# Scores three steps ahead of their values in the last cross attention, with six tiles of exponentials and a smaller arena

## The chip, the cores and the metric

The kernel runs on one core of one Trainium2 chip, in one launch. The metric is device time in microseconds; the kernel before takes 1653.15 us, the median of 3 runs (1653.11 to 1653.16). The engines are named as in the profile: PE is TensorE's matmuls, PEld its weight loads, DVE is VectorE, ACT is ScalarE, POOL is GpSimd, SP issues the transfers.

## The reference, cut to what matters

Four blocks follow each other on x of 8 batches x 112 rows x 256. Each attends to the same context of 8 x 375 x 192. All is in float32.

```python
x = L0(x, ctx)   # self attention, cross attention, gated GELU feed-forward; 16 heads of 64
x = L1(x, ctx)   # the same, other weights
x = L2(x, ctx)   # cross attention alone, 16 heads of 64
x = L3(x, ctx)   # decoder block, 16 heads of 16:
    # h = ln(x);  q, k, v = h @ qkv_w + qkv_b
    # a = softmax(where(causal | tgt_mask, -inf, q k^T * 0.25)); x += (a v) @ proj_w + proj_b
    # h = ln(x);  q = h @ q_w + q_b; k, v = ctx @ k_w + k_b, ctx @ v_w + v_b
    # a = softmax(where(enc_mask, -inf, q k^T * 0.25));          x += (a v) @ out_w + out_b
    # h = ln(x);  x += gelu(h @ mlp1_w + mlp1_b) @ mlp2_w + mlp2_b
```

## The kernel before, in words

The parts of the four blocks are numbered as stages 0 to 9: 0, 1, 2 are self attention, cross attention and feed-forward of the first block; 3, 4, 5 those of the second; 6 is the third block's cross attention; 7, 8, 9 are self attention, cross attention and feed-forward of the last. Attention is cut into *steps* (`add_step`, lines 913 to 1101). A step is a batch and some heads: in the cross stages four heads, so 32 steps a stage; in stage 7 eight heads, two steps a batch. The steps of stage 7 are woven between those of stages 6 and 8 (`after`, line 1194). In all there are 176 steps; step 138 is the first of stage 8 and step 175 the last.

A step has these items. "S" makes the scores on TensorE into two PSUM tiles "s" (a pool of two) and then issues the softmax. In stages 7 and 8 that is, for each head, a DVE instruction that adds the mask to the scores and takes the maximum (line 934; it writes the masked scores into an SBUF tile "pr" and the maximum into "nm"), and an exponential on ACT, in place (line 942). Half of a step's exponentials are issued with S, the other half in the item "E". "T" transposes the exponentials on TensorE, four heads to a bank, three banks in a cross step (line 1013), into PSUM tiles "mm" (a pool of four that every other product shares), and each bank is copied to an SBUF tile "wT": banks 0 and 2 by ACT (line 1022), bank 1 by DVE (line 1019). "PV" multiplies by the values (line 1043); two steps' PV stand together. After the last step of a batch, "R" and "N" scale the result by the sums. Step i uses two tiles of "pr"; the pool has four.

TensorE's instructions stay in the order in which the Python code emits them. That order is written by a planner (`Plan`). Its main loop (lines 1454 to 1495) goes step by step, and in loop step i it emits S(i+2), then the two PV if i is odd, then the banks of T(i+1), then E(i+2). Between these it puts *fill*: the other work (projections, layer norm transposes, feed-forward) by deadline, counted in steps, as soon as its inputs are there and there is room. `pace` says how much fill a step should take. The other engines' instructions follow each in its own queue, in an order close to that of emission.

Queries, keys and values live in one SBUF tile, the "arena", 12224 columns of float32 on 128 partitions. `Plan.find` gives each a place when its projection is emitted; a projection that finds no room has to wait. A cross stage with heads of 64 has for each batch eight keys of 375 columns and six values of 512.

The context masks of stage 8 are made on POOL ("mask" items, line 578); deadlines of queries (`q_deadline`), of the transposed layer norms "hT" (`hT_by`) and of the keys (`add_key_jobs`) are so many steps ahead of the step that uses them. The GELU of stage 9 is done for the feed-forward's first 512 rows and for the next 256 as separate ACT instructions over four banks of 512 or 256 columns (line 1325). They need another table of functions than the exponentials, so the first of them may only follow the last S in the plan:

```python
deps=[(("ff", st, f, m), 1.0) for m in range(8)] + [(("S", len(steps) - 1), 4.0)],
```

Of the kernel before, what the change touches and what calls it, by code (L numbers as in the profile page):

```python
# [15 lines left out]
B, T, D = 8, 112, 256  # L16
S, DC = 375, 192
# [46 lines left out]
def last_batch(t):  # L64
    return min(B - 1, (P * (t + 1) - 1) // T)
# [234 lines left out]
def kernel(ctx: ExitStack, tc: tile.TileContext, a: dict, out: bass.AP):  # L300
    nc = tc.nc
    PSUM = bass.MemoryType.PSUM
    RINGS = {"w": 7, "row": 2, "xn": 3}
    ARENA = 12224

    const = ctx.enter_context(tc.tile_pool(name="const", bufs=1))
    wpool = ctx.enter_context(tc.tile_pool(name="wpool", bufs=RINGS["w"]))
    rpool = ctx.enter_context(tc.tile_pool(name="rpool", bufs=RINGS["row"]))
    ppool = ctx.enter_context(tc.tile_pool(name="ppool", bufs=4))
    tpool = ctx.enter_context(tc.tile_pool(name="tpool", bufs=6))  # L310
    xpool = ctx.enter_context(tc.tile_pool(name="xpool", bufs=RINGS["xn"]))
    small = ctx.enter_context(tc.tile_pool(name="small", bufs=4))
# [4 lines left out]
    def mm_tile():  # L317
        return ps_m.tile([P, 512], F32, tag="mm", name="mm")

    arena = const.tile([P, ARENA], F32, name="arena")  # L320
    plan = Plan(RINGS, ARENA, lambda k: 512 if k[0] == "v" else S if k[0] == "k" and k[1] in (1, 4, 6, 8) else 4 * T)

    def place(key):

        lo, hi = plan.place[key]
        t = arena[:, lo:hi]
        return t if hi - lo != 4 * T else t.rearrange("p (i t) -> p i t", i=2)

    SEG = [0, 0, 0, 1, 1, 1, 2, 2, 2, 2]
# [216 lines left out]
    def add_masks():  # L546


        src = ("w", "m8")

        def load():
            m8 = wpool.tile([T, B * (T + S)], U8, tag="w", name="m8")
            nc.sync.dma_start(m8[:, : B * T], a["mask_BxS_bf0"].rearrange("b t -> (b t)").partition_broadcast(T))
            nc.sync.dma_start(m8[:, B * T :], a["mask_BxS2_bf0"].rearrange("b s -> (b s)").partition_broadcast(T))
            got[src] = m8

        def self_mask():
            nc.gpsimd.tensor_scalar_mul(cmask.rearrange("p b t -> p (b t)"), got[src][:, : B * T], NEG)
            nc.gpsimd.affine_select(
                cmask, cmask, pattern=[[0, B], [-1, T]], compare_op=ALU.is_ge, fill=NEG, base=0,  # L560
                channel_multiplier=1,
            )

        plan.add_load(Item(("load", "masks"), 0, load, makes=[src]))
        plan.add(Item(("mask", "self"), 0, self_mask, first_of(7, 0) - 8, uses=[src], seg=SEG[6]))
        yield
        for i in range(2):
            key = ("w", "cm", i)

            def place(i=i, key=key):  # L570
                got[key] = wpool.tile([T, 4, S], F32, tag="w", name="cm")

            plan.add_load(Item(("load", key), 0, place, makes=[key]))
            for n in range(4):

                def ctx_mask(i=i, n=n, key=key):
                    c = B * T + (4 * i + n) * S
                    nc.gpsimd.tensor_scalar_mul(got[key][:, n, :], got[src][:, c : c + S], NEG)

                b = 4 * i + n  # L580
                plan.add(Item(("mask", b), 0, ctx_mask, first_of(8, b) - 5, uses=[src, key], seg=SEG[7]))


    xns = {}
# [194 lines left out]
    def add_key_jobs(st, b, w, deadline, last=False):  # L779

        cols = slice(b * S, (b + 1) * S)
        wv = ("ctx", "k") if last else w
        rest = D if last else INNER
        for u in range(1 if last else 4):
            keys = [("k", st, b, 2 * u + i) for i in range(2)]
            cell = []

            def begin(u=u, cell=cell):
                for i in range(2):
                    ps = mm_tile()  # L790
                    nc.tensor.matmul(  # L791
                        ps[:, :S], lhsT=got[wv][:, (2 * u + i) * P : (2 * u + i + 1) * P], rhs=ctxA[:, cols],
                        start=True, stop=False,
                    )
                    cell.append(ps)

            def fn(u=u, keys=keys, cell=cell):
                for i in range(2):
                    r = slice(i * KB, (i + 1) * KB)
                    nc.tensor.matmul(  # L800
                        cell[i][:, :S], lhsT=got[wv][r, rest + u * P : rest + (u + 1) * P], rhs=ctxB[r, cols],
                        start=False, stop=True,
                    )
                for i in range(2):
                    t = place(keys[i])
                    evac(t, cell[i][:, :S], S, None, bcols[:, 6 + i : 7 + i] if last else None)
                    got[keys[i]] = t

            plan.add(Item(("kj", st, b, u), 2.1, fn, deadline(b, u), uses=[w], makes=keys, deps=ctx_deps(b),
                          seg=SEG[st], begin=begin))  # L810
# [36 lines left out]
    def ctx_deps(b):  # L847
        return [(("ctxT", b), 4.0)]
# [60 lines left out]
    at = {}  # L909
# [257 lines left out]
    def first_of(st, b):  # L1167
        return at[(st, b, 0)]

    def last_of(st, b):  # L1170
        return at[(st, b, per[st] - 1)]
# [6 lines left out]
        return lambda t: [(("N", st, last_batch(t)), 1.2)]  # L1178

    def q_deadline(st, j):  # L1180
        return first_of(st, 2 * j) - 3.4

    L0 = ("L0_xattn_", "Wq1 Wk1 Wv1 Wo1 bo1 g1 b1 Wq2 Wk2 Wv2 Wo2 bo2 g2 b2 Wp Wf bf g3 b3 bp".split())
    L1 = (
# [24 lines left out]
    def hT_by(st):  # L1209
        if st == 9:  # L1210
            return lambda gi: last_of(8, last_batch(GROUPS[gi][-1])) + 2.0
        if st in ff_at:
            return lambda gi: ff_at[st] - 0.5 + 0.02 * gi
        return lambda gi: first_of(st, (256 * gi) // T) - 4

    def norm_by(st):
        f = hT_by(st)
        if st == 9:
            return lambda t: last_of(8, last_batch(t)) + 1.4
        if st in ff_at:  # L1220
            return lambda t: f(t // 2) - 0.01
        return lambda t: f(t // 2) - 0.7
# [14 lines left out]
    def cross_stage(st, wq, wk, wv, qscale, vscale):  # L1237
        last = st == 8
        for j in range(4):
            if last:  # L1240
                add_last_projection(st, "q", j, wq, ("sq", "qc"), q_deadline(st, j), 2)
            else:
                add_pair_projection(st, "q", j, wq, 4, lambda j, u: q_deadline(st, j) + 0.01 * u, qscale)
        for b in range(B):

            add_key_jobs(st, b, wk, lambda b, u: at[(st, b, u)] - 3.0, last)
            if not last:
                add_value_jobs(st, b, wv, lambda b, i: at[(st, b, (0, 0, 2)[i])] - 1.5 + 0.1 * i, vscale)

        if last:  # L1250
            add_last_values(st, wv, lambda b: first_of(st, b) - 1.3)
# [102 lines left out]
    st = 0  # L1354
    for bi, (L, n) in enumerate(seq):
# [40 lines left out]
        if bi == 0:  # L1396
            add_context_transposes(lambda b: f1 + 4 * b - 5 if b > 1 else 7 + b)
        cross_stage(s1, w(n[7]), w(n[8]), w(n[9]), 0.125, None)
        add_products(s1, s2, w(n[10]), 8, after_pv(s1), norm_by(s2))
        add_norm_transposes(s2, n[17], n[18], hT_by(s2))  # L1400
# [50 lines left out]
    nc.vector.tensor_copy(vcols, pt0[:, :NVR])  # L1451
    plan.now = 7.0

    cuts = [0, ff_at[2], ff_at[5], ff_at[9]]
    for seg in range(3):
        lo, hi = cuts[seg], cuts[seg + 1]


        for s in (lo, lo + 1):
            for k in plan.items[("S", s)].uses + plan.items[("PV", s)].uses:  # L1460
                mk = plan.maker.get(k)
                if mk is None or plan.items[mk].done:
                    continue
                if plan.items[mk].begin is not None:
                    plan.require(mk)
                else:
                    plan.drain(mk)
        if seg == 0:
            plan.require(("hT", 0, 1))
        for i in range(lo - 2, hi):  # L1470
            plan.step = i
            left = plan.pace(i, seg)
            if i < lo:

                left = max(left, 6.5)
            plan.close_jobs()
            if lo <= i + 2 < hi:
                plan.main(("S", i + 2))

            if lo <= i < hi and (i - lo) % 2 == 1:  # L1480
                plan.main(("PV", i - 1))
                plan.main(("PV", i))
            if lo <= i + 1 < hi:
                n = steps[i + 1]
                share = left / (n + 2)
                left -= plan.fill(2 * share, 1.5 if i < lo else 0.0)
                for k in range(n):
                    plan.main(("T", i + 1, k))
                    left -= plan.fill(min(left, share))
            if ("E", i + 2) in plan.items and lo <= i + 2 < hi:  # L1490
                plan.main(("E", i + 2))
            plan.fill(left, 1.5 if i < lo else 0.0)


            plan.open_jobs(1 if i + 1 >= first_of(8, 0) or i + 2 in woven else 2, i + 3.5, seg)
# [38 lines left out]
```

## Time and profile before

| | |
|---|---|
| median of 3 runs | 1653.15 us |
| profiled execution: its own time | 1654.93 us |
| profiled execution: span from first to last instruction | 1653.1 us |
| busy: PE, PEld | 1633.3 us, 1141.0 us |
| busy: DVE, ACT, POOL | 812.8 us, 782.6 us, 718.5 us |
| granted TensorE clock, mean | 0.999 |
| step 138's scores start | 1423.9 us |
| step 175's scores start | 1603.5 us |

A line of a group reads: source line, engine, operation, out<-in with shapes, count, then busy us and mean ns of one, then idle time of the engine just before them and what ended it. A line of the waits reads: engine, tile and line that waited, what it waited for, then us in total, number of times, and the longest. A line of the timeline reads: start us, duration us, engine, line, operation, and in brackets the idle time before it with its releaser. A matmul's end in the profile is modelled, so a busy PE can hold short waits inside it; PEld, the weight load that precedes each matmul, often shows them better.

### The profile page before, as it was taken

How to read it: one execution, taken by the hardware profiler on the slowest of the kernel's cores; microseconds unless marked ns; L12 is line 12 of the kernel's file. 1: busy time of each engine (PE TensorE's matmuls, PEld its weight loads, DVE VectorE, ACT ScalarE, POOL GpSimd, SP SyncE). 2: the span in 40 equal slices, each digit the busy share in tenths (PEclk: the TensorE clock that was granted, in tenths of full speed). 3: DMA queues.
4: the chain of work that ended last, by engine and by line, in shares of the span. 5: the costliest groups of instructions: out<-in, count | busy, mean ns of one | idle time of the engine just before them, and what ended most of it. 6: DMA issues, size and time to landing. Idle time of an engine off the chain costs nothing.

```text
span 1653.1 us, 30104 instructions
## 1 busy us (share of the span) xinstructions
PE 1633.3 (99%) x11772; PEld 1141.0 (69%) x11772; DVE 812.8 (49%) x2164; ACT 782.6 (47%) x2450; POOL 718.5 (43%) x687
## 2 busy tenths in 40 slices
PE   9999999999999999999999999999999999999999
PEld 8777766666657878676666665675666666766667
DVE  3554454544532344545444552344455556677752
ACT  3453444444531445434444452144445555787772
POOL 1323555656632223355565570364564447422110
PEclk9999999999999999999999999999999999999999
DMA  6021020000101011000000010100000000000000
GB/s 187 5 66 42 3 87 1 1 26 1 52 29 46 1 29 52 27 1 30 1 2 26 1 46 30 33 23 1 1 2 1 16 2 26 30 2 1 2 2 23
DMA packets 26613, 39.50 MB, mean 24 GB/s; under 512 B 1527, under 2 KB 21623, under 8 KB 26471
## 3 DMA queue, kind: packets, MB, share of 16 engines
q1 hardware_dynamic: 26231, 37.40, 7.3%
q8 instruction: 93, 1.52, 0.4%
q14 instruction: 49, 0.40, 0.1%
q10 hardware_dynamic: 240, 0.17, 0.0%
HBM read 35.88 MB, written 0.92 MB: 22 GB/s over the span
## 4 chain that ended last, share of the span: by engine, by line
PE 91%; ACT 4%; DVE 3%; POOL 1%; issue 1%; ACTq 0%; POOLq 0%; DVEq 0%
PE mm L669 13%; PE mm L703 11%; PE mm L1043 10%; PE s L986 10%; PE mm L1013 9%; PE mm L791 8%; PE mm L825 7%; PE mm L1263 6%; PE mm L800 5%; PE mm L834 4%; PE mm L750 3%; ACT pr L942 2%; PE mm L1298 2%; PE mm L637 1%; ACT pr L954 1%
## 5 line engine op out<-in xcount | busy, mean ns | idle before, releaser
L963 POOL TENSOR_SCALAR pr<-pr,rinv 112x375 f32<-112x375 f32 x384 | 468.7, 1239 | 340.6 <-DVE rinv L960 340.6
L954 ACT ACTIVATE pr<-s,nm 112x375 f32<-112x375 f32 (+1 forms) x640 | 302.0, 490 | 168.7 <-DVE nm L948 166.5
L355 DVE COPY arena<-mm 128x375 f32<-128x375 f32 (+4 forms) x189 | 113.3, 609 | 287.8 <-PE mm L800 138.3
L1013 PEld LDWEIGHTS mm<-ident,pr 112*128 112x128 f32 (+2 forms) x1920 | 209.1, 151 | 48.1 <-issue 20.6
L1013 PE MATMUL mm<-ident,pr 112*128 112x112 f32 (+2 forms) x1920 | 234.7, 264 | 5.5 <-ACT pr L942 3.3
L347 ACT COPY arena<-mm 128x375 f32<-128x375 f32 (+4 forms) x179 | 92.8, 519 | 296.3 <-PE mm L800 140.9
L948 DVE TENSOR_REDUCE nm<-s 112x2 f32<-112x750 f32 (+1 forms) x224 | 206.3, 957 | 50.2 <-PE s L986 46.5
L986 PE MATMUL s<-arena 64*112 64x375 f32 (+3 forms) x1792 | 211.0, 394 | 0.1
L1043 PEld LDWEIGHTS mm<-wT,arena 128*64 128x64 f32 (+5 forms) x3840 | 160.5, 130 | 36.9 <-issue 19.0
L347 ACT COPY wT<-mm 119x448 f32<-119x448 f32 (+2 forms) x235 | 123.9, 536 | 124.5 <-PE mm L1013 124.4
L1043 PE MATMUL mm<-wT,arena 128*64 128x112 f32 (+5 forms) x3840 | 180.3, 262 | 0.0
L986 PEld LDWEIGHTS s<-arena 64*112 64x112 f32 (+1 forms) x1792 | 114.1, 172 | 80.4 <-issue 30.9
L942 ACT ACTIVATE pr<-pr,nm 112x112 f32<-112x112 f32 (+1 forms) x256 | 124.7, 491 | 32.0 <-DVE nm L934 32.0
L969 POOL TENSOR_TENSOR pr<-pr,rinv 112x896 f32<-112x896 f32 x32 | 53.9, 1685 | 197.5 <-DVE rinv L967 180.0
L954 ACT ACTIVATION_READ_ACCUMULATOR pr<-s,nm 112x1 f32 x640 | 133.3, 208 | 0.0
L599 POOL TENSOR_TENSOR rs<-ve,mhalf 128x1 f32<-128x1 f32 x70 | 39.7, 568 | 203.0 <-DVE ve L597 202.9
L960 DVE RECIPROCAL rinv<-sums 112x1 f32<-112x1 f32 x384 | 62.4, 163 | 90.1 <-ACT pr L954 89.6
L825 PE MATMUL mm<-L_xattn_Wv,ctxA 128*128 128x512 f32 (+1 forms) x192 | 92.5, 601 | 2.3 <-ACT wT L347 1.3
L791 PE MATMUL mm<-ctxA,L_xattn_Wk 128*128 128x375 f32 x256 | 92.0, 482 | 0.6 <-DVE wT L355 0.5
L673 DVE TENSOR_TENSOR x<-mm,x 128x256 f32<-128x256 f32 x70 | 29.6, 423 | 115.9 <-PE mm L669 115.9
L703 PE MATMUL mm<-hT,L_xattn_Wq 128*128 128x224 f32 x384 | 83.0, 360 | 0.0
L353 DVE TENSOR_SCALAR arena<-mm 128x448 f32<-128x448 f32 (+2 forms) x65 | 42.0, 646 | 82.0 <-PE mm L834 47.1
(134 smaller groups left out, 2323.7 us busy)
## 6 DMA issues: line engine op xcount, KB each, us to landing
L_xattn_Wo<-in_L_xattn_Wo_dram SPq DMA_DIRECT2D x3, 1024.0 KB, 15.8
L_xattn_w_ff<-in_L_xattn_w_ff_dram SPq DMA_DIRECT2D x3, 1024.0 KB, 5.2
L_xattn_Wv<-in_L_xattn_Wv_dram SPq DMA_DIRECT2D x4, 512.0 KB, 5.0
L_xattn_Wq<-in_L_xattn_Wq_dram SPq DMA_DIRECT2D x2, 1024.0 KB, 4.7
L_xattn_Wp<-in_L_xattn_Wp_dram SPq DMA_DIRECT2D x2, 1024.0 KB, 5.8
L_xattn_wq<-in_L_xattn_wq_dram SPq DMA_DIRECT2D x2, 1024.0 KB
L_xattn_wo<-in_L_xattn_wo_dram SPq DMA_DIRECT2D x2, 1024.0 KB, 5.2
L_xattn_mlp_w<-in_L_xattn_mlp_w_dram SPq DMA_DIRECT2D x2, 1024.0 KB, 5.4
```

Of the source, the lines that this page charges most:

```text
L347: nc.scalar.copy(dst, src)
L669: nc.tensor.matmul(ps[:, :D], lhsT=oT[:, c, t * P : (t + 1) * P], rhs=got[wv or w][:, c, :], start=(c == 0), stop=(c == n - 1),)
L703: nc.tensor.matmul(ps[:, i * 2 * T : (i + 1) * 2 * T], lhsT=got[w][:, k, m * P : (m + 1) * P], rhs=hT[:, k, lo:hi], start=(k == 0), stop=( ...
L791: nc.tensor.matmul(ps[:, :S], lhsT=got[wv][:, (2 * u + i) * P : (2 * u + i + 1) * P], rhs=ctxA[:, cols], start=True, stop=False,)
L825: nc.tensor.matmul(ps[: KCH[c][1], :], lhsT=lhs(ctxA, slice(0, KA), c), rhs=got[w][:, hf * 512 : (hf + 1) * 512], start=True, stop=False,)
L942: return nc.scalar.activation(pr, pr, AF.Exp, bias=nm, scale=-1.0, accum_out=bsums[(st, b)][:, h : h + 1])
L948: nc.vector.tensor_reduce(nm[:, :, :ns], sv, AX.X, ALU.max, negate=True)
L954: nc.scalar.activation(pr[:, bk, sl, :], sv[:, bk, sl, :], AF.Exp, bias=nm[:, bk, sl : sl + 1], accum_out=sums[:, bk, sl : sl + 1],)
L963: nc.gpsimd.tensor_scalar_mul(pr[:, bk, sl, :], pr[:, bk, sl, :], rinv[:, bk, sl : sl + 1])
L986: nc.tensor.matmul(tiles[i][:, n % 2, (n // 2) * nk : (n // 2 + 1) * nk], lhsT=qap(h), rhs=kap(h), start=True, stop=True,)
L1013: nc.tensor.transpose(pt[:kl, m * T : (m + 1) * T], cell[h][:, c * P : c * P + kl], ident[:T, :T])
L1043: nc.tensor.matmul(po[p0 : p0 + dp, blk * T : (blk + 1) * T], lhsT=got[vk][:kl, hv * dp : (hv + 1) * dp], rhs=wt, start=(c == 0 and par(h) ...
```

## The change

From loop step DEEP on (three before the first step of stage 8, so step 135) the planner emits S and E of step i+3 in loop step i instead of those of step i+2. On the first such step it emits both S(i+2) and S(i+3). In the stages before, nothing changes in this rule. For it the pool of "pr" tiles has six instead of four (a tile is 896 columns in its largest use), and the arena shrinks from 12224 to 10400 columns, in all stages. Deadlines of what stages 7 and 8 need before their scores are one step earlier: masks, queries, hT and keys.

```diff
-    ARENA = 12224
+    ARENA = 10400
...
-    ppool = ctx.enter_context(tc.tile_pool(name="ppool", bufs=4))
+    ppool = ctx.enter_context(tc.tile_pool(name="ppool", bufs=6))
...
-        plan.add(Item(("mask", "self"), 0, self_mask, first_of(7, 0) - 8, uses=[src], seg=SEG[6]))
+        plan.add(Item(("mask", "self"), 0, self_mask, first_of(7, 0) - 9, uses=[src], seg=SEG[6]))
...
-                plan.add(Item(("mask", b), 0, ctx_mask, first_of(8, b) - 5, uses=[src, key], seg=SEG[7]))
+                plan.add(Item(("mask", b), 0, ctx_mask, first_of(8, b) - 6, uses=[src, key], seg=SEG[7]))
...
     def q_deadline(st, j):
-        return first_of(st, 2 * j) - 3.4
+        return first_of(st, 2 * j) - (4.4 if st > 6 else 3.4)
...
-        return lambda gi: first_of(st, (256 * gi) // T) - 4
+        return lambda gi: first_of(st, (256 * gi) // T) - (5 if st > 6 else 4)
...
-            add_key_jobs(st, b, wk, lambda b, u: at[(st, b, u)] - 3.0, last)
+            add_key_jobs(st, b, wk, lambda b, u: at[(st, b, u)] - (4.0 if last else 3.0), last)
...
+    DEEP = first_of(8, 0) - 3
...
-            if lo <= i + 2 < hi:
-                plan.main(("S", i + 2))
+            ahead = 3 if seg == 2 and i >= DEEP else 2
+            due = [n for n in range(i + 2, i + ahead + 1) if lo <= n < hi and not plan.items[("S", n)].done]
+            for n in due:
+                plan.main(("S", n))
...
-            if ("E", i + 2) in plan.items and lo <= i + 2 < hi:
-                plan.main(("E", i + 2))
+            for n in due:
+                if ("E", n) in plan.items:
+                    plan.main(("E", n))
```

## The prediction

> **What bounds the kernel now.** I read the page first, then stretches of ten to thirty us of the last block, then who waits for whom in them, and last the instructions around two of the waits. Part 1 of the page gives busy time by engine, part 4 the chain that ended last:
>
> ```profile
> PE 1633.3 (99%) x11772; PEld 1141.0 (69%) x11772; DVE 812.8 (49%) x2164; ACT 782.6 (47%) x2450; POOL 718.5 (43%) x687
> PE 91%; ACT 4%; DVE 3%; POOL 1%; issue 1%; ACTq 0%; POOLq 0%; DVEq 0%
> ```
>
> TensorE bounds the whole; its matmul work is untouched by the change, so only time in which it stands can be won. The stretches (columns: busy us of PE, PEld, DVE, ACT, POOL, then granted clock) show where that is:
>
> ```profile
> 1424.00:1444.00 20.00, 19.31 (x208) 14.05 (x209) 15.24 (x56) 15.15 (x44) 8.15 (x10) 1.00 0.19 60
> 1444.00:1464.00 20.00, 18.84 (x209) 14.04 (x208) 16.30 (x73) 18.64 (x69) 4.45 (x9) 1.00 0.01 2
> 1564.00:1594.00 30.00, 30.00 (x234) 17.07 (x231) 15.25 (x53) 19.61 (x51) 3.42 (x7) 1.00 0.00 1
> 1594.00:1604.00 10.00, 9.24 (x115) 6.52 (x113) 7.78 (x27) 9.34 (x28) 0.25 (x1) 1.00 0.01 2
> 1604.00:1614.00 10.00, 8.19 (x133) 6.34 (x126) 5.38 (x18) 7.76 (x15) 2.92 (x4) 0.83 0.01 2
> ```
>
> ACT is at 93% in places (18.64 of 20), with room just before (15.15 of 20). TensorE's waits from 1424 to 1598 (stage 8 up to its last three steps), and for contrast those of stage 4:
>
> ```profile
> PE mm L1013 <- ACT pr L942: 2.0, 7, 0.4
> PE mm L791 <- ACT wT L1022: 1.1, 2, 0.6
> PE mm L866 <- ACT wT L1022: 0.7, 3, 0.3
> PE mm L669 <- ACT wT L1022: 0.5, 1, 0.5
> ```
> ```profile
> PE mm L825 <- DVE wT L355: 0.5, 2, 0.2
> PE mm L1263 <- ACT gate L1270: 0.2, 1, 0.2
> ```
>
> Two kinds: a transpose (L1013) waits for an exponential (L942), and a matmul waits for a PSUM tile that ACT has still to copy (L1022). The earlier cross stages hardly wait. Durations, from the groups of this stretch by form:
>
> ```profile
> L942 ACT ACTIVATE pr<-pr,nm 112x375 f32<-112x375 f32 x128 | 76.6, 602 | 25.8 <-DVE nm L934 25.8
> L934 DVE CUSTOM_DVE_ANT_0 pr<-s,cm 112x375 f32<-112x375 f32 x128 | 62.6, 542 | 7.2 <-PE s L986 6.3 <-ACT pr L942 0.5
> L1022 ACT COPY wT<-mm 128x448 f32<-128x448 f32 x32 | 16.6, 518 | 2.5 <-PE mm L1013 2.5
> L1013 PE MATMUL mm<-ident,pr 112*128 112x112 f32 x256 | 35.0, 265 | 3.7 <-ACT pr L942 3.3 <-ACT wT L1022 0.2
> ```
>
> One such place, and the tail, in order of time:
>
> ```profile
> 1459.95 0.32 PE L1013 MATMUL mm<-ident,pr 112*128 112x112 f32 x1 [0.40 <-ACT pr L942]
> 1461.57 0.95 ACT L1022 COPY wT<-mm 128x448 f32<-128x448 f32 x2
> 1462.14 1.13 PE L669 MATMUL mm<-squares,oT 128*128 128x256 f32 x4 [0.48 <-ACT wT L1022]
> ```
> ```profile
> 1608.28 0.32 PE L1013 MATMUL mm<-ident,pr 112*128 112x112 f32 x1 [0.71 <-ACT pr L942]
> 1610.63 1.28 ACT L1325 ACT_TABLE_LOAD   x1
> 1611.92 3.71 ACT L1325 ACTIVATE oT<-oT 128x2048 f32<-128x2048 f32 x2
> ```
>
> A matmul's idle time understates a wait, since its modelled end is stretched over it. Taking instead the distance from each matmul's start to the next, less what the same pair usually has, the waits from 1424 to 1598 come to 9.0 us: 4.6 for exponentials, 3.8 for copies, 0.6 other.
>
> **The change, step by step.** *One step more of lead.* With matmul groups at their row durations (scores 0.83, a bank of four transposes 0.45, values 0.65 a step), the work that stands on TensorE between a step's scores and its first transpose in stage 8 and the woven steps of stage 7 goes, by the order of the built programs, from 2.6-16.6 us (eight of 38 steps under 4.1) to 4.9-24.4 (none). What the path needs is about 4.1: 0.54 + 0.08 for the first masked maximum, four exponentials at 0.60, two copies at 0.53 between them. So I take away all 4.6 us of waits for exponentials: -4.6 (bounds 0, where ACT itself is the limit, and -4.6).
>
> *What is late next.* ACT runs in order, and now has the first half of step i+3's exponentials, not i+2's, ahead of the copies of step i+1's transposes. A transpose no longer held back fills its PSUM tile (four "mm" tiles) sooner and meets the copy instead. Between two copies ACT owes the same work as before; it only starts a step earlier. That helps where it idled before the crowd (4.85 of 20 us from 1424), not inside it (1.36 of 20 from 1444). Bounds on the 3.8 us: all gone, or grown by the 4.6 just removed. I take a third gone: -1.3, nearer to no change because the queue's order is the same.
>
> *Entry.* At DEEP two score steps are made back to back. Step 138 needs both "s" tiles, held by step 137 until its eight masked maxima of 112 columns are done: eight at 0.19 (their start-to-start in the timeline), so +1.5, plus the pipeline. The query evacuations of batch pair 0 now precede it by less, 3.5 us of TensorE work, under the same wait. Something of the 1.1 us lost at 1428-1430 goes with the lead. Bounds 0 and +2.5; I take +1.4.
>
> *Tail.* Step 175's scores come a step earlier, so the planner sees the first GELU of stage 9 as possible inside the last step: the built ACT queue has, after one copy of step 174, the table load and the two 2048-wide GELUs, and only then three copies of steps 174 and 175. Before, they came after every copy. Counting from the scores of step 174 by rows: TensorE ends T175 at 11.2; ACT ends its copy at 9.65, GELU at 9.65 + 1.28 + 3.71 = 14.65, the copies at 16.2; the last values end at 16.6, then hT and output tile 0, which now stands ahead of the feed-forward: 18.9. Before, the same starting point to the feed-forward's first product took 14.9 us (1598.87 to 1613.77), without 4.4 us of work that now lies inside (one pair of values 1.30, transposes 1.35, output tile 1.73): 19.3. So -0.4 at full clock: the wait for exponentials is replaced by one for GELU.
>
> The clock adds to it. In the trace it is 0.50 from 1610.3 to 1613.7, after TensorE stood for most of 1607-1609, and the values took 2.10 instead of 1.29, the hT transposes 1.11 instead of 0.59. The new wait is longer in one piece (some 4 us), so I put the same 1.3 on it: tail +0.9 in all (bounds -4.4, if every tail wait went, and +2.5).
>
> The Trainium skill, "TensorE: Matmul & The Clock Gate", section "What's actually happening", says the clock is halved after one idle window of about 3.4 us and is given back after about 3.4 us of work; it speaks against this change, as it makes one long wait dearer than several short ones. By the page's 3.4 us at half clock alone the term would be an estimate of +1.7 rather than +1.3, and the sum 0.4 us longer.
>
> *Smaller arena.* 12224 to 10400 columns changes the planner's order in stages 1, 4 and 6. The lead of a key projection over its scores falls from a median of 29 us of TensorE work to 26-27 (shortest 15.2 to 10.3), of a value projection over its use from 23.7 to 16.9 at the shortest; an evacuation takes 0.6. Nothing is late, so 0; bounds -2 and +6, as the pairs of open projections meet other copies (stages 1 and 4 lose 2.1 and 0.7 us to waits now). *Six exponential tiles* are what three steps of two need; the "nm" maxima have four, so step i+3's wait for step i+1's exponentials, which T(i+1) waited for anyway: 0. *Masks, hT, queries, keys one step earlier*: the same distance to scores that also moved: 0; the mask work is POOL's, 3.42 busy of 30 us late in the stage. No DMA is issued more; SP's loads are released by the same ring of seven tiles.
>
> Sum: -4.6 - 1.3 + 1.4 + 0.9 = -3.6. The profiled span of 1653.1 agrees with the median of 1653.15 (that execution's own time, 1654.9, has 1.8 around its span), so 1649.5.
>
> **Rivals.** *B, the wait changes its name:* where ACT is full, waits for exponentials become waits for L1022 copies. For it: 18.64 of 20 us busy; against: 145.6 of the 190 us from 1424 to 1614. Half of the 4.6 returns and no copy wait goes: -2.3 + 1.4 + 0.9 = 0, 1653. *C, slower, by the arena:* in the 96 cross steps of stages 1, 4 and 6 opened projections bunch and meet uncopied tiles. Each such wait has the size of the L825 rows (0.2, with its weight load up to 1.1). It decides from about 7 us in all, 0.07 us a step; at 0.09 us a step it adds 8.6: 1658. For it: the order differs in hundreds of rows; against: leads above 10 us. *D, ACT was only late, not short:* all 9.0 go, with a tail of +0.9 and an entry of +0.5: 1645.5.
>
> **How the numbers follow.** A (1649.5) 0.40, B 0.28, C 0.20, D 0.12. About 0.2% (3.3 us) is what a measurement tells from no change. A lies at that bound, and some of it falls inside: faster 0.46, same 0.33, slower 0.21. The range reaches from D's value to near C's: 1645 to 1657.5; A's own is 1647.5 to 1651.
>
> **What would show it.** Right: no wait of L1013 for L942 between 1424 and 1598; busier TensorE in 1444-1464; a wait of about 1.5 us for L934 before step 138's scores; ACT_TABLE_LOAD before three of the last L1022 copies and TensorE standing some 4 us before the last values, then clock 0.5. Wrong: L1013's waits gone but L669, L791 and L866 waiting for L1022 as much more (B); new waits in stages 1, 4 and 6, whose stage lengths should stay within 1 us (C).

## The result, and the profile after

The changed kernel takes **1663.25 us** (median of 6 runs, 1660.9 to 1665.9), the kernel before, beside it, 1653.16 us (1653.09 to 1654.79). The ratio is 1.0056, with a 95% interval of 1.0045 to 1.0066: 10 us slower, where 3.6 us less had been forecast. The profiled execution took 1664.03 us, 1661.9 of them between its first and last instruction; that of the kernel before took 1654.93 and 1653.1.

Part 1 of the page after, busy time by engine, and part 4, the chain that ended last:

```profile
PE 1635.1 (98%) x11772; PEld 1143.4 (69%) x11772; DVE 816.5 (49%) x2159; ACT 785.0 (47%) x2455; POOL 718.4 (43%) x687
PE 90%; ACT 4%; DVE 3%; issue 1%; POOL 1%; ACTq 0%; POOLq 0%; DVEq 0%
```

The work is the same; 8.8 us more pass in which TensorE stands or runs slowly. Who waited for whom, after, from 1430 to 1607 us, which is stage 8 up to its last three steps (columns: waiter, what it waited for, us in all, times, longest):

```profile
PE mm L866 <- ACT wT L1022: 4.9, 5, 2.0
PE mm L866 <- DVE x L673: 1.0, 1, 1.0
PE mm L1089 <- DVE oT L1054: 0.5, 1, 0.5
PE mm L791 <- ACT wT L1022: 0.4, 1, 0.4
```

Before, L1013 waited for exponentials (L942) 2.0 us here; no such line is left. But the waits for copies (L1022) have grown from 2.3 us to 5.3. By form, after, from 1432 to 1607 us:

```profile
L942 ACT ACTIVATE pr<-pr,nm 112x375 f32<-112x375 f32 x118 | 70.7, 602 | 24.1 <-DVE nm L934 24.1
L1022 ACT COPY wT<-mm 128x448 f32<-128x448 f32 x29 | 15.1, 520 | 2.8 <-PE mm L1013 2.7
L1013 PE MATMUL mm<-ident,pr 112*128 112x112 f32 x232 | 29.0, 262 | 0.0
```

Neither the exponentials nor the copies became slower (602 and 520 ns each, 602 and 518 before). The stretches after (busy us of PE, PEld, DVE, ACT, POOL, then the granted clock):

```profile
1444.00:1464.00 20.00, 19.29 (x273) 14.94 (x272) 15.83 (x75) 18.23 (x68) 4.45 (x9) 1.00 0.01 2
1594.00:1604.00 10.00, 10.00 (x88) 5.84 (x76) 5.61 (x20) 6.86 (x18) 0.00 (x0) 1.00 0.00 0
1604.00:1614.00 10.00, 9.72 (x164) 8.03 (x157) 7.66 (x27) 9.43 (x27) 1.90 (x3) 1.00 0.01 3
1614.00:1624.00 10.00, 5.87 (x63) 4.96 (x62) 1.89 (x4) 5.37 (x6) 0.95 (x2) 0.66 0.00 0
```

The last row is the new hole: TensorE busy 5.87 of 10 us, at a clock of 0.66. The tail in order of time:

```profile
1613.09 1.28 ACT L1325 ACT_TABLE_LOAD   x1
1614.38 3.71 ACT L1325 ACTIVATE oT<-oT 128x2048 f32<-128x2048 f32 x2
1618.00 1.38 ACT L1022 COPY wT<-mm 119x448 f32<-119x448 f32 x3
1618.56 2.47 PE L1043 MATMUL mm<-wT,arena 128*32 128x112 f32 x48 [4.13 <-ACT wT L1022]
1620.96 1.12 PE L637 MATMUL mm<-ident,xn 128*128 128x128 f32 x4
```

Three copies stand behind the table load and the two GELUs, and the last values wait 4.13 us for them, as the prediction had read from the queue. And the entry, where step 137's scores (112 columns) and step 138's (375) meet:

```profile
1413.86 0.32 PE L1013 MATMUL mm<-ident,pr 112*128 112x112 f32 x1 [0.90 <-POOL pr L963]
...
1417.36 0.66 PE L986 MATMUL s<-arena 32*112 32x112 f32 x16
1419.08 1.66 PE L986 MATMUL s<-arena 32*112 32x375 f32 x8 [1.06 <-DVE nm L934]
```

The second wait was forecast; the first one, of step 135's transposes for POOL, was not (0.19 us in the kernel before).

**Lost time by stretch.** To set kernels with different orders side by side, I took for each matmul the distance from its start to the next one's, less the usual distance of its form (the 30th percentile over all kernels here), and added this up between the ends of the values of given steps. A matmul that starts late, through a wait or a slow clock, shows as lost time wherever it stands in the order. Differences to the profile of before, in us, counted to the last matmul, so that a sum can lie up to 0.4 under the difference of the spans; the steps are 65 (in stage 4), 113 (stage 6), 135 and 139 (the entry), 171 (the tail begins). The kernels of the rows are told below.

```
                 to 65  65-113  113-135  135-139  139-171  171-end    sum
after             -0.4    +0.5     +5.9     -0.4     +2.5     +0.8   +8.8
memory            -0.9    +0.8     -0.1     +0.1     +1.5     -1.0   +0.5
deadlines         -0.4    +0.4     +3.2      0.0     +0.8     -1.3   +2.7
lead_only         -0.6    +0.8     +2.6     -0.5     -0.2      0.0   +2.2
mended             0.0    +0.8     -0.1     +1.9     -0.2     -5.1   -2.6
spread             0.0    +0.8      0.0     +1.1     -0.9     -4.9   -4.0
```

The first column differs by this much between runs without a cause. In the last one -1.2 is what a kernel has whose profile lacks the stretch of half clock that the profile of before shows at 1610. One execution stands behind each row, so a few tenths mean nothing. After loses between steps 113 and 139 (+5.5, where the earlier deadlines and the entry both fall) and in the middle (+2.5), not in one place.

### The profile page after: what moved, and what is told of

It reads as the page before. It is cut to its first block, busy times and chain, and to the rows that moved or that the text cites. A ratio compares the mean times of both kernels' runs of the same rounds, so it can differ in the third digit from the quotient of the medians.

```text
span 1661.9 us, 30252 instructions
## 1 busy us (share of the span) xinstructions
PE 1635.1 (98%) x11772; PEld 1143.4 (69%) x11772; DVE 816.5 (49%) x2159; ACT 785.0 (47%) x2455; POOL 718.4 (43%) x687
## 4 chain that ended last, share of the span: by engine, by line
PE 90%; ACT 4%; DVE 3%; issue 1%; POOL 1%; ACTq 0%; POOLq 0%; DVEq 0%
PE mm L669 12%; PE mm L703 11%; PE s L986 10%; PE mm L1043 10%; PE mm L1013 9%; PE mm L791 8%; PE mm L825 7%; PE mm L1263 6%; PE mm L800 5%; PE mm L834 4%; PE mm L750 3%; ACT pr L942 2%; PE mm L1298 2%; PE mm L725 1%; DVE nm L948 1%
## 5 line engine op out<-in xcount | busy, mean ns | idle before, releaser
L1013 PEld LDWEIGHTS mm<-ident,pr 112*128 112x128 f32 (+2 forms) x1920 | 208.5, 151 | 43.3 <-issue 20.5
L1013 PE MATMUL mm<-ident,pr 112*128 112x112 f32 (+2 forms) x1920 | 232.5, 263 | 2.4 <-POOL pr L963 0.9
L942 ACT ACTIVATE pr<-pr,nm 112x112 f32<-112x112 f32 (+1 forms) x256 | 124.7, 491 | 30.0 <-DVE nm L934 30.0
L673 DVE TENSOR_TENSOR x<-mm,x 128x256 f32<-128x256 f32 x70 | 29.6, 423 | 119.3 <-PE mm L669 119.3
```

What stands on the lines that cost most here:

```text
L942: return nc.scalar.activation(pr, pr, AF.Exp, bias=nm, scale=-1.0, accum_out=bsums[(st, b)][:, h : h + 1])
L1013: nc.tensor.transpose(pt[:kl, m * T : (m + 1) * T], cell[h][:, c * P : c * P + kl], ident[:T, :T])
```

## The experiments

All of them compute the whole of the reference. Beside them, on the same chip, the kernel before took 1654.3 us (memory, deadlines, gelu_last, copies_first), 1654.06 (lead_only, mended, hT_queries, keys), 1653.7 (lead_late, lead_tail and the two with copies on DVE) and 1653.6 (lead_all, spread, before_spread); ratios are to those.

### Parts of the change alone

**memory**: the kernel before with the smaller arena and six tiles.

```diff
-    ARENA = 12224
+    ARENA = 10400
...
-    ppool = ctx.enter_context(tc.tile_pool(name="ppool", bufs=4))
+    ppool = ctx.enter_context(tc.tile_pool(name="ppool", bufs=6))
```

> The kernel before with only the two sizes changed: an arena of 10400 columns and six exponential tiles; scores stay two steps ahead and all deadlines are the old ones. Theory 1 (the loss of 10 us comes from three places of the last block: the entry of two score steps in a row, copies that stand behind exponentials in ACT's queue, and the GELU ahead of the last copies): the sizes cost little, about what the trace of the changed kernel shows by step 129, +0.9; 1653 to 1655. Theory 2 (the planner's new order under the smaller arena is what costs): most of the loss is here already, 1659 or more.

Measured: 1654.64 us, ratio 1.0003 (0.9993 to 1.0012). Rival C, slower by the arena, falls. A trace of it is there: from step 65 to 113 every kernel with the small arena but one (lead_all, below) loses 0.4 to 0.9 us more than the kernels with the large one; the time cannot tell that from nothing.

**deadlines**: the changed kernel with two steps of lead, so that the deadlines and the memory remain.

```diff
-            ahead = 3 if seg == 2 and i >= DEEP else 2
+            ahead = 2
```

> The changed kernel with the lead put back from three steps to two; the small arena, the six tiles and the earlier deadlines of masks, queries, hT and keys stay. Theory 1: no entry, no GELU in front, so 1653 to 1656, like the run with the two sizes alone. Theory 2, or a variant in which the earlier deadlines crowd out the work that hides the exponentials: 1658 or more.

Measured: 1658.25 us, ratio 1.0024 (1.0015 to 1.0034). The deadlines, which I had put at nothing, cost 4 us. Waits of this kernel from 1255 to 1418 us, stages 6 and 7:

```profile
PE mm L825 <- ACT wT L347: 1.2, 3, 0.7
PE mm L791 <- DVE wT L355: 0.9, 2, 0.5
PE mm L1013 <- POOL pr L963: 0.9, 1, 0.9
```

In the same stretch of the kernel before, these three are 0.6, 0.5 and 0.2 us: several waits grew a little. Two further runs have half of it each. **hT_queries** is "deadlines" with keys and masks as before:

```diff
-    add_key_jobs(st, b, wk, lambda b, u: at[(st, b, u)] - (4.0 if last else 3.0), last)
+    add_key_jobs(st, b, wk, lambda b, u: at[(st, b, u)] - 3.0, last)
...
```

**keys** is "deadlines" with hT, queries and masks as before:

```diff
-        return first_of(st, 2 * j) - (4.4 if st > 6 else 3.4)
+        return first_of(st, 2 * j) - 3.4
...
-        return lambda gi: first_of(st, (256 * gi) // T) - (5 if st > 6 else 4)
+        return lambda gi: first_of(st, (256 * gi) // T) - 4
...
```

> The kernel that has the earlier deadlines and two steps of lead (1658.3), with the deadlines of keys and masks as before, so only hT, its norms and the queries of stages 7 and 8 come a step earlier. Theory 'stage 7's queries and hT, pulled into stage 6, break its order': nearly all of the 4 us stay, about 1657.5, and +2.1 at step 121 and +3 at 135 are seen again. Rival 'the keys of stage 8 crowd the woven steps': 1654.5, milestones of before until 137.

> The other half: only the keys of stage 8 a step earlier, two steps of lead, hT, queries and masks as before. Theory 'hT and queries': 1654.5, within 1 us of the kernel before. Rival 'keys': about 1657.5, with the loss after step 133.

Measured: hT and queries 1657.25 us, ratio 1.0017 (1.0008 to 1.0027), with 1.9 us lost between steps 113 and 135; keys 1655.37 us, ratio 1.0008 (0.9998 to 1.0018). So most of it is hT and queries: with them alone the first two of the waits above are there in full (1.2 and 0.9 us), with the keys alone they are 0.5 and 0.5. My reading is that fill taken earlier is missing as cover where a transpose or a projection then meets an unfinished POOL or ACT; that is argued from the waits, and no run shows it. With hT and queries alone the POOL wait is 0.2 us, so the 0.9 us needs more than them.

**lead_only**: the changed kernel with every deadline as before; lead, tiles and arena stay.

```diff
-        return first_of(st, 2 * j) - (4.4 if st > 6 else 3.4)
+        return first_of(st, 2 * j) - 3.4
...
-        return lambda gi: first_of(st, (256 * gi) // T) - (5 if st > 6 else 4)
+        return lambda gi: first_of(st, (256 * gi) // T) - 4
...
-    add_key_jobs(st, b, wk, lambda b, u: at[(st, b, u)] - (4.0 if last else 3.0), last)
+    add_key_jobs(st, b, wk, lambda b, u: at[(st, b, u)] - 3.0, last)
...
```

> The changed kernel with every deadline as before (masks, hT, queries, keys); three steps of lead, six tiles and the small arena stay. Theory 'the parts add': the earlier deadlines cost 4.0 us in the run that had them alone, so this one is 4 faster than the changed kernel, about 1659.5, and the 5 us left over the kernel before sit at the first deep step (about +2) and in the tail (+2.6). Rival 'the lead needs its earlier deadlines': the inputs of scores that stand one step earlier arrive late, waits for arena tiles of queries and keys appear from step 137 on, and the time is 1663 or more. In both the milestones up to step 133 are those of before within 0.5 us.

Measured: 1658.5 us, ratio 1.0026 (1.0016 to 1.0037). The parts add: the deadlines' 4 us and this run's 4.4 make 8.4 of the 10, and the old deadlines make nothing late. And the lead alone wins nothing in the middle (-0.2 from step 139 to 171). Its waits from 1424 to 1600:

```profile
PE mm L866 <- ACT wT L1022: 2.8, 5, 0.9
PE mm L791 <- ACT wT L1022: 1.9, 4, 0.7
PE mm L866 <- DVE x L673: 1.0, 1, 1.0
```

The exponentials' waits are gone, and 4.7 us for copies stand where the kernel before had 2.3 for copies and 2.0 for exponentials.

### The tail and the entry

**gelu_last**: the changed kernel with the first GELU held until the last step's transposes.

```diff
-   deps=[(("ff", st, f, m), 1.0) for m in range(8)] + [(("S", len(steps) - 1), 4.0)],
+   deps=[(("ff", st, f, m), 1.0) for m in range(8)] + [(("S", len(steps) - 1), 4.0), (("T", len(steps) - 1, 2), 0)],
```

> The changed kernel with one more dependency in the plan: the first GELU of stage 9 may only follow the last bank of transposes of step 175, so ACT makes the last three copies before the table load and the GELU. Theory 1: TensorE's wait of 4.1 us before the last values goes, and most of the half clock behind it; the time falls by 3 to 5 us, to about 1659. Rival (the end is bound by the last exponentials and copies, and a wait of the old kind takes the place): less than 1 us.

Measured: 1661.4 us (1657.83 to 1661.96), ratio 1.0036 (1.0023 to 1.0049). That is 2 us more than expected, but its runs differ in the granted clock as those of after do (last section): at a mean clock of 0.999 it took 1657.8 us, after 1660.9 and 1661.3. The long wait of the tail is gone; its last values (columns as in the timelines above) now start without a wait and at full clock:

```profile
1618.32 1.36 PE L1043 MATMUL mm<-wT,arena 128*32 128x112 f32 x48
1619.62 0.66 PE L637 MATMUL mm<-ident,xn 128*128 128x128 f32 x4
```

1.36 instead of 2.47 us, 0.66 instead of 1.12. From step 171 on, this kernel loses 5.1 us less than the kernel before, 3.9 of it without the half clock in that one's profile: in the tail the lead does what it was meant to. The profiled run lost 2.8 us more than after between steps 113 and 135, where it ran at half clock for 6.8 us, so its sum says little.

**mended**: lead_only, with gelu_last's edit, and the second score step at DEEP issued behind the transposes of that loop step.

```diff
-            for n in due:
-                plan.main(("S", n))
+            for n in due[:1]:
+                plan.main(("S", n))
...
+            for n in due[1:]:
+                plan.main(("S", n))
             for n in due:
                 if ("E", n) in plan.items:
```

> The run with old deadlines, and two more edits: at the first deep step the second score step is issued after the transposes of that step, not directly behind the first, and the first GELU is held until the last step's transposes. Theory 'deadlines, entry and tail are the whole loss, and the middle gains nothing because ACT is full': about 1655, within 2 us of the kernel before and not under it by more than 1. Rival 'the lead gains its 4.6 us of exponential waits once the losses are away': 1650 or less.

Measured: 1652.73 us, ratio 0.9992 (0.9982 to 1.0001). Less than expected by 2 us, and by the interval not yet faster than before. The table says where: the tail wins 5.1 (1.2 of it the half clock in the profile of before), the entry still costs 1.9 (two steps later), the middle gives nothing.

**lead_late** and **lead_tail**: the same with the lead begun at step 159, or at 171, and the second score step put between values and transposes (the edit for lead_late; lead_tail has `first_of(8, 7) - 1`).

```diff
-    DEEP = first_of(8, 0) - 3
+    DEEP = first_of(8, 4) - 1
```

> As the run that came out at 1652.7 (old deadlines, first GELU held for the last transposes), but the third step of lead begins only when batch 4 of the last stage begins, after the steps woven with stage 7, with its extra score step put between the values and the transposes of that step. Theory 'the lead is worth nothing in the middle, costs its entry (2.0 us between steps 135 and 139) and wins in the tail (-5.0 us after step 171 in that run)': entry gone, tail kept, so 2 below it, about 1650.5. Rival 'the entry only shifts a score step and is free, the middle won what the entry lost': 1652.5 or more.

> The same with the third step of lead from the last batch (step 171) on alone. Theory 'only the tail wins': the same as the run with the late lead, about 1650.5, within 0.7 us of it. Rival 'late in stage 8, where ACT is two thirds busy, the lead does remove waits': 1 us or more behind that run.

Measured: 1652.45 us, ratio 0.9991 (0.9983 to 1.0), and 1653.28 us, ratio 0.9996 (0.9988 to 1.0005). The entry did not go; it moved. Lead_late loses 1.5 us more than before between 139 and 171, all of it between 159 and 161, where it begins, and its tail wins the same 5.1. Lead_tail wins 2.3 there, entry included. My theory that a late entry is free was wrong.

**lead_all**: mended, with three steps of lead from the segment's first step (96) on.

```diff
-            ahead = 3 if seg == 2 and i >= DEEP else 2
+            ahead = 3 if seg == 2 else 2
```

> The 1652.7 run with three steps of lead from the first step of the last segment (step 96) on, so there is no entry at step 135: the extra score step is made at the segment's start, where feed-forward products stand as cover. Theory 'the entry is a real cost of 2 us, paid where a step's eight maxima stand between two score steps': 135 to 139 as in the kernel before, 1650.5. Rival 'the entry is paid wherever it is made, or keys and queries of stage 6 come late for the lead': 1652.5 or more.

Measured: 1657.11 us, ratio 1.002 (1.0012 to 1.0029); again the rival. Steps 135 to 139 are those of before, but 7.9 us are lost between 65 and 113. One wait there, at the segment's start (waits from 1050 to 1250):

```profile
PE s L986 <- ACT pr L954: 3.0, 1, 3.0
```

and behind it half clock (busy us of PE, then the clock):

```profile
1074.00:1081.00 7.00, 6.40 (x18) 0.51 0.00 0
```

In stage 6 the exponentials read the scores from PSUM, so the third score step waits for them and not for the maxima alone. An extra score step needs the two "s" tiles free once more than the rhythm gives, wherever it stands: 1.1 to 2.1 us in stages 7 and 8 by the table and lead_late, some 7 us in stage 6, of which 3.0 are the wait and most of the rest the half clock behind it. That the "s" tiles are the whole of it is read from the two waits, not tried.

### Why the middle gains nothing

**copies_first**: the changed kernel with no exponential of a step from 139 on, of stage 8 or of the stage-7 steps among it, right behind its scores, but all in E, behind the copies of that loop step.

```diff
-            for _ in range(len(late) // 2):
+            for _ in range(len(late) // 2 if s <= first_of(8, 0) else 0):
```

> The changed kernel with all exponentials of a step, from step 139 on, issued in the item E, behind the copies of the transposes, instead of half of them with S, in front. Theory 1: with three steps of lead the exponentials are not urgent and the copies are, so the waits for L1022 copies (5.3 us in sum by the waits from 1424 to 1606) fall to under 2 and the time falls by 3 to 5 us, to about 1659. Rival (ACT is simply full in the crowded stretches, whatever its order): the waits stay or return as waits for exponentials, under 1 us of change.

Measured: 1663.17 us, ratio 1.0058 (1.0041 to 1.0075), as after. Waits from 1430 to 1607:

```profile
PE mm L866 <- ACT wT L1022: 4.1, 5, 1.7
```

The copies' waits fell from 5.3 to 4.1 us, not under 2 as expected, and no time was won by this order. I concluded that ACT is simply full in the crowded stretches, and tested it:

**copies_on_DVE**: mended, and in the odd steps of batches 0 to 2 of stage 8 the third copy goes to DVE. **before_copies** has the same six copies moved in the kernel before.

```diff
-            if dh == 16 and i == 1:
+            if dh == 16 and (i == 1 or (i == 2 and st == 8 and s % 2 and b < 3)):
```

> The 1652.7 run (lead from step 138 on), and in the odd steps of batches 0 to 2 of the last stage the third copy of transposes goes to VectorE in place of ScalarE (six copies of 0.52 us). Theory 'ScalarE, full in the crowded stretch, is what turns waits for exponentials into waits for copies': the 4.7 us of waits for L1022 copies fall by a half or more and the time by 2 to 3, to about 1650. Rival 'the order in the queues, not the sum of work': VectorE's copy stands behind four masked maxima, waits move to it, 1652 to 1655.

> The kernel before (two steps of lead) with the same six copies moved to VectorE and nothing else. Theory 'ScalarE full': waits for exponentials and copies between steps 139 and 157 fall by 2 us, 1652 beside 1654 for the kernel before. Rival 'with two steps of lead the chain from scores to transposes is too short whoever copies': within 0.7 us of the kernel before.

Measured: 1651.92 us, ratio 0.9989 (0.998 to 0.9998), and 1654.17 us, ratio 1.0004 (0.9995 to 1.0013). The busiest stretch of the kernel before with the copies moved:

```profile
1444.00:1464.00 20.00, 18.84 (x209) 14.13 (x208) 17.39 (x78) 17.99 (x69) 4.44 (x9) 1.00 0.01 2
```

ACT fell from 18.64 to 17.99 us, DVE rose, and TensorE's 18.84 stayed. The waits from 1424 to 1598 stayed too:

```profile
PE mm L1013 <- ACT pr L942: 2.0, 7, 0.4
PE mm L791 <- ACT wT L1022: 1.1, 2, 0.6
PE mm L866 <- ACT wT L1022: 0.7, 3, 0.3
```

These are the numbers of the kernel before, to the digit. Mended has the two copy lines of lead_only above (2.8 and 1.9 us), and copies_on_DVE has the same two. So less work on ACT shortened no wait. The test is a small one, though. The six moved copies stand between 1436 and 1503 us and cannot touch the later waits; they are third copies of a step, behind the first one, for which the matmul shown below waits; and the planner, which gives some other copies to the engine that it takes to be freer, put two key evacuations (line 343, 0.57 us) back on ACT, so that only some 2 us left it. It speaks against ACT's sum of work as the limit, as rival B had it and I had come to believe, and does not exclude it. What else can matter is where a copy stands in the queue. TensorE and ACT in mended, around the longest wait for a copy:

```profile
1516.32 1.40 PE L1013 MATMUL mm<-ident,pr 112*128 112x112 f32 x12
1519.02 0.70 PE L866 MATMUL mm<-ctx_w,ctxA 128*128 128x256 f32 x2 [0.85 <-ACT wT L1022]
```
```profile
1516.07 0.61 ACT L942 ACTIVATE pr<-pr,nm 112x375 f32<-112x375 f32 x1
...
1516.68 0.60 ACT L942 ACTIVATE pr<-pr,nm 112x375 f32<-112x375 f32 x1
...
1517.27 0.60 ACT L942 ACTIVATE pr<-pr,nm 112x375 f32<-112x375 f32 x1
...
1517.86 0.60 ACT L942 ACTIVATE pr<-pr,nm 112x375 f32<-112x375 f32 x1
...
1518.45 0.94 ACT L1022 COPY wT<-mm 128x448 f32<-128x448 f32 x2
```

Four exponentials in a row, 2.4 us, stand ahead of the two copies, the second half of step i+2's and the first half of step i+3's, and only four "mm" tiles are there for all products: three hold the transposes, the first two instructions of L866 take the fourth, and the next two wait until the first copy is made (it ends just before 1519.0). Copies_first kept four in a row too, in another place. So:

**spread**: mended, with two exponentials of a stage-8 step behind each of ACT's two copies. **before_spread** has the same in the kernel before.

```diff
-            for _ in range(len(late) // 2):
+            lates[s] = late
+            for _ in range(len(late) // 2 if s < first_of(8, 0) else 0):
                 late.pop(0)()
...
                 for k in range(n):
                     plan.main(("T", i + 1, k))
                     left -= plan.fill(min(left, share))
+                    for m in due[:1]:
+                        if m >= first_of(8, 0):
+                            for _ in range(len(lates[m]) // (n - k + 1)):
+                                tc.keep_in_program_order(lates[m].pop(0)())
```

> The 1652.7 run (old deadlines, lead of three from step 138, entry staggered, first GELU held), with the exponentials of stage 8's steps, and of the stage-7 steps among them, spread: none right behind their scores, but for a step of the last stage two behind each of ScalarE's two copies. Before that four stand together ahead of the first copy. Theory 'what the lead lost in the middle is the queue: a copy stands behind four exponentials (2.4 us) whatever the sum of ScalarE's work': waits for L1022 copies, 5.0 us in that run, fall to 2.5 or less without exponential waits coming back; 1650 (1649 to 1651). Rival 'the four mm tiles are too few for any order': waits of the same sum, within 0.7 us of 1652.5.

> The kernel before, two steps of lead, with the same spreading and nothing else. If the spreading needs the lead: the last two exponentials of a step come too close to its own transposes, waits of L1013 for L942 rise from 3.3 us, time 1654 to 1657. If only the queue's order counted and the lead nothing: 1651 or less.

Measured: spread **1650.96 us** (1650.12 to 1651.62), ratio 0.9984 (0.9975 to 0.9993): the best version, faster than both kernels, than the kernel before by 2.6 us. All its eleven runs are below all ten of mended. TensorE makes the same 11772 matmuls in the same order in mended, copies_on_DVE and spread; what differs is the queues of the other engines. The same place in spread, where the lines from 994 on are one further down:

```profile
1516.12 1.40 PE L1014 MATMUL mm<-ident,pr 112*128 112x112 f32 x12
1517.36 1.31 PE L866 MATMUL mm<-ctx_w,ctxA 128*128 128x256 f32 x4
```
```profile
1516.20 0.62 ACT L942 ACTIVATE pr<-pr,nm 112x375 f32<-112x375 f32 x1
...
1516.81 0.60 ACT L942 ACTIVATE pr<-pr,nm 112x375 f32<-112x375 f32 x1
...
1517.40 0.52 ACT L1023 COPY wT<-mm 128x448 f32<-128x448 f32 x1
```

The first copy starts 1.3 us behind the first transpose instead of 2.1, and L866 goes through without a wait. Waits from 1427 to 1600:

```profile
PE mm L866 <- ACT wT L1023: 1.0, 2, 0.8
PE mm L866 <- DVE x L673: 0.8, 1, 0.8
...
PE mm L791 <- ACT wT L1023: 0.6, 2, 0.3
```

Waits for copies, with 0.4 of L1014's, are 2.0 us, in mended 4.7; all listed waits of the stretch are 5.3 us, in mended 7.1. The exponentials and copies on ACT are as many as in mended; the planner moved three key evacuations from ACT to DVE and one query evacuation back, some 1.2 us, which is less than what copies_on_DVE had taken off ACT without effect. So here it is the order. The wait for L673 (1.0 us in mended, 0.8 in spread) stays: at 1541 us in mended that instruction starts on DVE right behind three masked maxima, which the spreading does not move. The time that the waits give back is smaller, 0.7 us in the middle and 0.8 at the entry by the table; the two ratios differ by 0.0008, or 1.3 us, and their intervals overlap. Before_spread took 1659.98 us, ratio 1.0043 (1.003 to 1.0055). Its first line of waits from 1424 to 1600:

```profile
PE mm L1014 <- ACT pr L942: 6.4, 17, 0.7
```

With two steps of lead the spread exponentials come too late for their own transposes (2.0 us in the kernel before). So this layout of ACT's queue needs the lead; and with it the lead is worth a little in the middle, 0.9 us by the one profile.

## Why the prediction was wrong

- **One step more of lead (-4.6): the waits went, the time did not.** "No wait of L1013 for L942 between 1424 and 1598" came true. But lead_only, which has the lead with the deadlines undone, changes the middle by -0.2.
- **What is late next (-1.3): this is the step that failed.** "Between two copies ACT owes the same work as before; it only starts a step earlier" is true of the sum and misses the order. I had seen that the first half of step i+3's exponentials stands ahead of step i+1's copies, had given the bound of +4.6 for it, and then taken a third of the copy waits as gone. In lead_only the copies' waits grow by 2.4 us, a little more than the 2.0 by which the exponentials' fall, and another 1.0 us is a wait for L673 on DVE. Rival B had the right name; its reason, ACT full, finds no support: some 2 us less work on ACT left the waits as they were, and nearly the same work in another order more than halved the copies'. The two terms together were off by 5.7 us.
- **Deadlines ("the same distance to scores that also moved: 0"): the other step that failed, by 4 us.** The scores of the ten steps of stage 7 ahead of step 138 did not move at all: the lead begins at loop step 135 with S(138), while their hT, queries and mask were put a step earlier from the start. The deadlines run loses +3.2 us between steps 113 and 135, before any step has its lead. Items are fill, and I compared distances of items to their users, not what the old place of an item loses; that this is how the time goes is argued, not shown.
- **Entry (+1.4):** right in kind and nearly in size. The wait for L934 is there, 1.06 us by the profile, and the two columns around the entry give +2.1 in lead_only. Moving it within stages 7 and 8 changed its cost little (1.1 to 2.1 us).
- **Tail (+0.9):** right, 4.13 us of wait for the forecast "some 4", the half clock behind it, +0.8 net. Not seen was that the rest of the tail wins about 5 with the GELU held (3.9 without the half clock in the profile of before): an edit of one dependence hid most of what the change could earn.
- **Smaller arena (0), six tiles (0):** right within what the time can tell; +0.4 to +0.9 us in stages 4 to 6 is there in the traces.
- **The clock, and the wait before it,** took the rest. After shows two stretches of half clock. The one in the tail was in the sum; the other, at 1504, follows a wait of 2.04 us for a copy (0.58 at that place in lead_only). Wait and half clock together cost the middle some 1.9 us that neither part has alone (2.5 against 0.8 and -0.2).

The sum again: -3.6 forecast, +5.7 middle, +4.0 deadlines, +0.7 entry, +1.9 clock and its wait, +0.1 arena and -0.1 tail make +8.7; the profiles differ by 8.8.

## What to carry to other kernels

Here a deeper lead took a wait away from the consumer of a chain and put it on what stands behind the producer's work in the same queue: write down what is ahead of each evacuation in that queue, before crediting the lead. Deadlines of fill are not free to move (4 us here); look also at the place that an earlier item leaves. A lead has an entry, where an extra step must find its buffers free, and it wins at the end, as long as nothing else is let into the place that it frees there; weigh these two first, as the steady middle may give nothing.

## What the runs showed of the hardware

The granted clock falls after waits shorter than I had allowed for. Stretches of the kernel after, PE alone (busy us, then the clock):

```profile
1500.00:1504.00 4.00, 2.18 (x32) 1.00 0.00 0
1504.00:1507.00 3.00, 2.78 (x8) 0.52 0.00 0
...
1616.00:1623.00 7.00, 4.44 (x55) 0.55 0.00 0
```

and of the kernel "memory", whose TensorE works in stage 8 in the order of the kernel before:

```profile
1458.00:1462.00 4.00, 2.92 (x22) 1.00 0.01 4
1462.00:1466.00 4.00, 3.92 (x8) 0.57 0.00 0
```

After, one wait of 2.04 us was followed by some 3.4 us at about half clock, the 4.13 us wait in the tail and the 3.0 us wait of lead_all each by about 7. In "memory" three waits of 0.40, 0.27 and 0.48 us within 3 us were enough; the kernel before has such waits at the same place in its profile, at full clock. So the short waits that the change removes carry a risk of half clock too, and it does not strike in every execution.

The Trainium skill, "TensorE: Matmul & The Clock Gate", section "What's actually happening", has the clock halved after an idle window of about 3.4 us and restored after about 3.4 us of work, with windows that run freely and don't start with the kernel. The lengths of about 3.4 and 7 us, and the same place at full clock in one profile and at half in another, agree with that. That the window must be idle does not: TensorE was busy 2.18 and 2.92 of the 4 us before. Deadlines, mended and spread show a mean clock of 1.000, after and gelu_last 0.997. The times of the runs go with their clocks. The six runs of the kernel after had a mean clock of 0.999 at 1660.9 and 1661.3 us, 0.998 at 1662.5 and 0.997 at 1664.0, 1664.9 and 1665.9; all eleven of spread had 1.000, within 1.5 us. A mean clock lower by 0.002 over 1660 us is an estimated 3.3 us, so the clock accounts for most of the 5 us between the runs of after; even its runs at 0.999 are over 6 us behind every run of the kernel before beside them.
